# Nineteen slices for twenty in the last run of a pair of embedding fields

## The chip, the core and the metric

The kernel runs on one core of a Trainium2 chip. The metric is the device time of one execution in microseconds. The engines are named as in the profile: PE is TensorE (PEld its weight loads), DVE is VectorE, ACT is ScalarE, POOL is GpSimd and SP is SyncE, which here only issues DMAs.

## What is computed

A wide-and-deep recommender forward pass for 16384 rows. Cut to what matters:

```
tok = word_emb[token_idx].mean(axis=1)        # 32 rows of a 50000 x 300 table
e1, e2, e3 = emb_mhN[mhN_idx].mean(axis=1)    # 20 rows each of 1000, 5000, 10000 x 64 tables
o1, o2, o3, o4 = emb_ohN[ohN_idx]             # one row each of 100, 50, 20, 1000 x 64 tables
emb  = concatenate([tok, e1, e2, e3, o1, o2, o3, o4], axis=1)      # 748 columns
wide = sum of the looked-up wide_* weights of all seven small fields
h = relu(emb @ W1 + b1); h = relu(h @ W2 + b2); h = relu(h @ W3 + b3)   # 748-1024-512-256
return sigmoid(h @ Wd + bd + wide)
```

## The kernel before

**Tiles and steps.** The 16384 rows are 128 tiles of 128 rows. One Python loop over `step` (L710) writes the whole program out in order, under a manual schedule[...]. A tile has STEPS = 11 steps (`t, i = divmod(step, STEPS)`), and WAKE = 27 more steps follow the last tile, so there are 1435 steps.

**Four streams share the steps.**

- *Tokens* (`tokens`, L285). The 32 word rows of a tile's 128 samples are gathered by indirect DMAs that POOL issues (L300), two to a group of `tok_rows`, with six such buffers; three groups later DVE adds them up (`add_up`, L276, L278, L283). There are 4034 gathers: 32 to a tile, and in every second tile from the fifth on one fewer, because SP fetches that row set with plain DMAs (L335). Groups are paced (`tokens_by`, L670): two a step in the first 24 steps, then (2051 − 48) / (1435 − 24) = 1.42 a step.
- *Counts.* For the small fields DVE makes one-hot rows from the keys (`one_hots`, L394, two buffers of `hot`), ACT scales a part of them (L401), PE multiplies them into counts per table row, six pairs of samples a step (`counts`, L412; four in step 10), and ACT writes the counts to SBUF as `cnt` (L415).
- *Small sums* (`small_sums`, L427, matmul on L447) are the stream that the change touches. While step i of tile t makes the counts of t, PE multiplies the finished counts of tile t − 1 with the tables on the chip. The tables lie in n_h = 138 slices of 128 rows: e1 8, o4 8, e2 40, e3 79, o1, o2 and o3 one each. Fields go in pairs in the order of `SMALL`: (e1, o4) 16 slices, (e2, e3) 119, (o1, o2) 2, and (o3) 1. Each pair sums into one PSUM tile `pg` from a pool with a single buffer, `ps_g` (L124); after the pair's last slice the generator yields an `evict`, a DVE reduce from `pg` into the features `g` (L437). The next pair's first slice is the next call of the generator, and its matmul waits for that reduce, since it writes the same buffer.
- *Layers.* The MLP works on blocks of three tiles (two and one near the end: 32 blocks of three, 12 of two, 8 of one), matmul by matmul (L565), with its results drained by ACT (L576). `layers.to(target + ahead)` (L772) sets how many are emitted in a step; `ahead` is the number of slices that an even spread would have done by then less those done.

**The order within a step:** `one_hots` of the next step; `counts` of this one; the early run of slices (L739); transposes of features where due (L488); token groups (L763); layer matmuls (L772); the late run of slices (L778); then `flush(step)` (L779) emits the reduces that are due. A reduce from an early run is due in the same step, one from a late run a step later (the last argument of `run_sums`). In step 0, `wide_term` of the tile before (L455, L461) comes right after this flush.

**How many slices each step has** is the table that the change edits (L636 to L643). `large` is 119 / 6 rounded up, 20:

```
step         1    2 (late)   3    4    5    6    7    9   10 (late)
slices      16    20        20   20   20   20   20    2    1
```

These are 139 for 138 slices. Pair (e2, e3) has 119 and begins in step 2; it takes 20 there, 80 in steps 3 to 6 and 19 in step 7. The twentieth slice of step 7 is o1's. Step 9 then has o2 and o3, and step 10 finds nothing left.

Of the kernel before, what the change touches and what calls it, by code (L numbers as in the profile page):

```python
# [74 lines left out]
def kernel(  # L75
# [560 lines left out]
    n_of = {f: slices[f][1] - slices[f][0] for f in SMALL}  # L636
    sizes_of_pairs = [sum(n_of[f] for f in SMALL[i : i + 2]) for i in (0, 2, 4, 6)]
    large = -(-sizes_of_pairs[1] // 6)
    early_sums = {1: sizes_of_pairs[0], 9: sizes_of_pairs[2], **{i: large for i in range(3, 8)}}
    late_sums = {2: large, 10: sizes_of_pairs[3]}  # L640
    sums_done = [0]
    for i in range(STEPS):
# [67 lines left out]
    for step in range(n_steps):  # L710
        t, i = divmod(step, STEPS)
# [129 lines left out]
```

## Time and profile before

| what | value |
|---|---|
| three timed runs | 5158.36, 5164.18, 5163.98 us, median 5163.98 us |
| profiled execution, its own time | 5157.98 us |
| profiled execution, span from first to last instruction | 5156.2 us |
| mean granted TensorE clock | 0.989 |
| PE busy | 4809.1 us (93%), 36252 matmuls |
| PEld busy | 3716.6 us (72%) |
| DVE busy | 3754.0 us (73%) |
| ACT busy | 2757.7 us (53%) |
| POOL busy | 3819.6 us (74%), 4034 of its 4041 instructions gathers |
| DMA engines | 44% in most slices, mean 127 GB/s |

The profile is one execution, which was 6.0 us shorter than the median of the timed runs and as long as the shortest of them. "Busy" counts instructions only[...]. Ends of matmuls are modelled, so that neighbours overlap. In timeline rows the columns are start, duration, engine, line, operation, output and inputs, and in brackets the idle time ahead with what ended it; rows of one kind in a row are merged, with their number after x.

### The profile page before, as it was taken

Reading aid. Unit: us, or ns where it says so; the run is one execution under the profiler, and the core shown is the slowest. Engines: PE = TensorE matmul, PEld = TensorE weight load, DVE = VectorE, ACT = ScalarE, POOL = GpSimd, SP = SyncE. Lnnn points to the kernel's source line nnn. Section 1 sums busy time; section 2 is a strip of 40 time slices with the busy share of each in tenths; the row PEclk is TensorE's granted clock in tenths of the full one; section 3 lists DMA queues with packets and bytes.
Section 4 is the critical chain, followed back from the end, with each engine's and each line's share of the span. In section 5 each row is a group of like instructions: output and inputs, shape, how many; then the busy total and the mean of one; then the engine's idle time right before and its main releaser. Section 6 shows DMA issues by size and latency. Waiting matters only on the chain.

```text
span 5156.2 us, 119649 instructions
## 1 busy us (share of the span) xinstructions
PE 4809.1 (93%) x36252; PEld 3716.6 (72%) x36252; DVE 3754.0 (73%) x6664; ACT 2757.7 (53%) x3658; POOL 3819.6 (74%) x4041
## 2 busy tenths in 40 slices
PE   6799999999999999999999999999999999999999
PEld 4566676676676667666667766766767888888898
DVE  6777777777777777777777777777777777777774
ACT  6455555555555555555555555555555555555552
POOL 7777777777777777777777777777777777777775
PEclk8899999999999999999999999999999999999999
DMA  7444444444444444444444444444444444444443
GB/s 202 128 126 126 123 127 127 124 126 124 125 127 123 124 127 124 125 126 125 125 125 126 125 126 123 127 128 127 127 128 124 126 125 124 128 127 127 127 120 100
DMA packets 276178, 653.78 MB, mean 127 GB/s; under 512 B 136091, under 2 KB 144667, under 8 KB 275527
## 3 DMA queue, kind: packets, MB, share of 16 engines
q0 software_dynamic: 193632, 619.88, 44.4%
q1 hardware_dynamic: 81895, 26.25, 2.4%
q8 instruction: 283, 4.64, 0.4%
q14 instruction: 368, 3.01, 0.2%
HBM read 645.63 MB, written 0.07 MB: 125 GB/s over the span
## 4 chain that ended last, share of the span: by engine, by line
PE 83%; DVE 9%; DMA 3%; issue 2%; ACT 2%; POOL 1%; SPq 1%; DVEq 0%; POOLq 0%; ACTq 0%
PE ph L565 44%; PE pg L447 28%; PE pc L412 8%; DMA tok_rows<-in_word_emb_dram,it 3%; DVE g L437 2%; DVE hot L394 2%; DVE own L278 2%; DVE own L283 2%; PE pc L488 2%; POOL tok_rows L300 1%; PE po L597 1%; DVE x L492 1%; ACT cnt L415 1%; ACT hot L401 0%; SPq L335 0%
## 5 line engine op out<-in xcount | busy, mean ns | idle before, releaser
L300 POOL DMA_INDIRECT tok_rows<-in_word_emb_dram,it x4034 | 3818.7, 947 | 1309.7 <-issue 907.9
L447 PE MATMUL pg<-terms,cnt 128*128 128x195 bf16 x17664 | 1735.9, 248 | 206.1 <-DVE g L437 206.1
L401 ACT ACTIVATE hot<-hot 64x768 bf16<-64x768 bf16 (+1 forms) x1408 | 1155.4, 821 | 1443.4 <-DVE hot L394 1427.5
L394 DVE TENSOR_TENSOR hot<-own,sc 128x1656 bf16<-128x1656 bf16 (+1 forms) x1408 | 1393.5, 990 | 367.9 <-PE pc L412 306.3
L447 PEld LDWEIGHTS <-cnt 128*128 128x128 fp8e3 x17664 | 1520.7, 98 | 43.2 <-issue 26.7
L565 PE MATMUL ph<-x,w_sb 128*128 128x384 f32 (+5 forms) x4932 | 1489.6, 441 | 45.8 <-DVE x L492 44.9
L415 ACT ACTIVATE cnt<-pc 128x828 uint16<-128x828 f32 (+1 forms) x1408 | 1186.9, 843 | 642.2 <-PE pc L412 615.0
L565 PE MATMUL ph<-h,w_sb 128*128 128x384 f32 (+2 forms) x4160 | 1219.6, 433 | 0.0
L565 PEld LDWEIGHTS ph<-x,w_sb 128*128 128x128 f32 (+1 forms) x4932 | 839.7, 192 | 454.9 <-issue 102.7
L278 DVE TENSOR_TENSOR own<-own,tok_rows 128x300 f32<-128x300 f32 x1920 | 917.5, 478 | 82.9 <-DMA tok_rows<-in_word_emb_dram,it 18.6
L565 PEld LDWEIGHTS ph<-h,w_sb 128*128 128x128 f32 x4160 | 700.4, 190 | 351.5 <-issue 103.8
L412 PEld LDWEIGHTS <-hot 128*128 128x128 bf16 x8192 | 592.0, 98 | 466.4 <-issue 220.7
L283 DVE TENSOR_TENSOR own<-own,tok_rows 128x300 f32<-128x300 f32 x1792 | 856.6, 478 | 94.3 <-DMA tok_rows<-in_word_emb_dram,it 33.3
L412 PE MATMUL pc<-hot 128*128 128x138 bf16 x8192 | 727.9, 224 | 55.8 <-ACT hot L401 53.5
L437 DVE TENSOR_REDUCE g<-pg 128x130 f32<-128x390 f32 (+1 forms) x512 | 262.1, 512 | 523.6 <-PE pg L447 518.2
L576 ACT ACTIVATE h<-ph,b_sb 128x384 f32<-128x384 f32 (+2 forms) x723 | 378.8, 524 | 274.6 <-PE ph L565 263.9
L492 DVE TENSOR_TENSOR x<-pc,scale 128x768 f32<-128x768 f32 x127 | 120.8, 951 | 105.8 <-PE pc L488 105.4
L381 DVE COPY sc<-pc 128x512 bf16<-128x512 bf16 x64 | 44.2, 691 | 144.4 <-PE pc L377 139.0
L488 PE MATMUL pc<-ident,g 128*128 128x128 f32 x762 | 106.7, 277 | 9.9 <-ACT cnt L415 9.9
L488 PEld LDWEIGHTS pc<-ident,g 128*128 128x128 f32 x762 | 83.0, 142 | 21.1 <-ACT cnt L415 16.8
L597 PE MATMUL po<-h,wd_sb 128*1 128x384 f32 (+2 forms) x208 | 70.0, 426 | 4.0 <-ACT h L576 2.7
L276 DVE TENSOR_TENSOR own<-tok_rows 128x300 f32<-128x300 f32 x128 | 61.3, 479 | 7.6 <-DMA tok_rows<-in_word_emb_dram,it 3.7
(54 smaller groups left out, 397.0 us busy)
## 6 DMA issues: line engine op xcount, KB each, us to landing
fetched<-in_word_emb_dram SPq DMA_DIRECT2D x7936, 1.2 KB
tok_rows<-in_word_emb_dram,it POOLq DMA_INDIRECT x4034
ix<-in_idx_dram SPq DMA_DIRECT2D x128, 32.0 KB
w_sb<-in_W_dram SPq DMA_DIRECT2D x6, 512.0 KB
raw<-in_mh_dram SPq DMA_DIRECT2D x4, 682.5 KB
it<-in_idx_dram SPq DMA_DIRECT2D x64, 32.0 KB
w_sb<-in_W_dram SPq DMA_DIRECT2D x1, 2048.0 KB
column<-in_idx_dram SPq DMA_DIRECT2D x62, 0.5 KB
```

Source lines behind the costliest of these rows:

```text
L278: nc.vector.tensor_add(tok_sum, tok_sum, a)
L283: nc.vector.tensor_add(to, tok_sum, b)
L300: nc.gpsimd.indirect_dma_start(out=rows[-1], out_offset=None, in_=word, in_offset=bass.IndirectOffsetOnAxis(ap=it[:, j : j + 1], axis=0),)
L394: nc.vector.tensor_tensor(hot[:, 0 : 2 * rows, :].rearrange("p i (n d) -> p i n d", d=2), iota.rearrange("p (n d) -> p n d", d=2).unsqueez ...
L401: nc.scalar.activation(upper, upper, AF.Copy, scale=UPPER)
L412: nc.tensor.matmul(pc[:, k // n, at : at + n_h], hot[:, 2 * k, 0:P], hot[:, 2 * k + 1, :], start=True, stop=True)
L415: nc.scalar.activation(cnt[:, :, b : b + rows].rearrange("l h (g k) -> l h g k", g=2), pc[:, :, 0 : n * n_h].rearrange("l g (k h) -> l h g ...
L437: nc.vector.tensor_reduce(field_columns(features(t), pair), pg[:, 0:n, :].rearrange("p f (c d) -> p f d c", c=3), AX.X, ALU.add,)
L447: nc.tensor.matmul(pg[:, j, :], by_slice[:, h, :], terms[:, h, :], start=(h == h0), stop=(h == h1 - 1))
L488: nc.tensor.transpose(pt[:, j // n, j % n, :], g[:, c : c + P], ident)
L565: nc.tensor.matmul(to, weights[: src.shape[0], k, m * P : (m + 1) * P], src, start=(k == 0), stop=(k == len(srcs) - 1),)
L576: nc.scalar.activation(dst[:, m, 0:n], ph[:, 0:n], AF.Relu, bias=bias[:, m : m + 1])
```

## The change

One entry of the table becomes a remainder. Step 7 has 119 − 5·20 = 19 slices instead of 20; everything else in the source is as it was.

```diff
     large = -(-sizes_of_pairs[1] // 6)
-    early_sums = {1: sizes_of_pairs[0], 9: sizes_of_pairs[2], **{i: large for i in range(3, 8)}}
+    early_sums = {1: sizes_of_pairs[0], 9: sizes_of_pairs[2], **{i: large for i in range(3, 7)}}
+    early_sums[7] = sizes_of_pairs[1] - 5 * large
     late_sums = {2: large, 10: sizes_of_pairs[3]}
     sums_done = [0]
     for i in range(STEPS):
```

The numbers now add up to 138. Step 7 ends with e3's last slice, step 9 has o1 and o2, and the late run of step 10 has o3. The counts of `sums_done`, which set `ahead`, are 135 and 137 after steps 7 and 9 where they were 136 and 138; step 10 ends at 138 in both.

## The prediction

> **What bounds the kernel now.** I read the page first, section 1 and the groups of section 5.
>
> ```profile
> PE 4809.1 (93%) x36252; PEld 3716.6 (72%) x36252; DVE 3754.0 (73%) x6664; ACT 2757.7 (53%) x3658; POOL 3819.6 (74%) x4041
> ...
> L300 POOL DMA_INDIRECT tok_rows<-in_word_emb_dram,it x4034 | 3818.7, 947 | 1309.7 <-issue 907.9
> L447 PE MATMUL pg<-terms,cnt 128*128 128x195 bf16 x17664 | 1735.9, 248 | 206.1 <-DVE g L437 206.1
> ```
>
> PE looks like the bound at 93%. Its largest idle time by far, 206.1 us, stands ahead of slice matmuls and ends with the pair reduce. The total of waits says how often:
>
> ```profile
> PE pg L447 <- DVE g L437: 206.1, 259, 6.2
> ```
>
> 259 times is twice per tile (128 tiles) and three more. The timeline of one tile shows both places, step 9 of one tile and step 7 of the next:
>
> ```profile
> 2503.62 0.24 PE L447 MATMUL pg<-terms,cnt 128*128 128x195 bf16 x1
> 2503.91 0.57 DVE L437 TENSOR_REDUCE g<-pg 128x130 f32<-128x390 f32 x1 [0.21 <-PE pg L447]
> 2504.53 0.24 PE L447 MATMUL pg<-terms,cnt 128*128 128x195 bf16 x1 [0.66 <-DVE g L437]
> ...
> 2535.60 1.80 PE L447 MATMUL pg<-terms,cnt 128*128 128x195 bf16 x19
> 2537.43 0.56 DVE L437 TENSOR_REDUCE g<-pg 128x130 f32<-128x390 f32 x1 [0.90 <-PE pg L447]
> 2538.05 0.24 PE L447 MATMUL pg<-terms,cnt 128*128 128x195 bf16 x1 [0.65 <-DVE g L437]
> ```
>
> In step 7, 19 slices run, PE stands while DVE empties `pg`, then o1's slice runs alone. In step 9, o2 runs, PE stands again, and o3 follows. All layer matmuls of the step queue behind.
>
> POOL at 74% looks idle, but its timeline is a fixed beat. The first and last gathers of the run, and one from the middle with its neighbour:
>
> ```profile
> 3.00 1.10 POOL L300 DMA_INDIRECT tok_rows<-in_word_emb_dram,it  x1 [1.52 <-DMA it<-in_idx_dram]
> ...
> 2499.11 0.94 POOL L300 DMA_INDIRECT tok_rows<-in_word_emb_dram,it  x1 [0.30 <-issue]
> 2500.36 0.95 POOL L300 DMA_INDIRECT tok_rows<-in_word_emb_dram,it  x1 [0.30 <-issue]
> ...
> 5128.90 0.95 POOL L300 DMA_INDIRECT tok_rows<-in_word_emb_dram,it  x1 [0.30 <-issue]
> ```
>
> A gather is 0.95 us and 0.30 us always stand ahead of it, whatever is named as releaser: 1.25 us. The windows of 250 us, which hold 200 beats, tell how full POOL is:
>
> ```profile
> core 0: us, POOL busy (x), PEclk, DMA share, GB/s
> 1000.00:1250.00 250.00, 185.18 (x196) 0.99 0.47 125
> 3500.00:3750.00 250.00, 189.29 (x200) 1.00 0.48 127
> ```
>
> From 3500 to 3750 not one beat is missed; elsewhere 2 to 5 of 200 are. From 5080.11 to 5128.90, 39 beats take 48.79 us, 1.251 each. So 4033 beats need 5041 to 5045 us, and took 5128.90 − 3.00 = 5125.90: **POOL has only 81 to 85 us of slack in the whole run.** Two engines are nearly full, and the change relieves one.
>
> [...] `pg` has one buffer, and the 0.66 us are what it costs here. [...]20 in a row take 1.89 us, (1.89 − 0.25) / 19 = 0.086 each.
>
> **The change part by part.**
>
> *Removed: two stands per tile.* In step 7 the twentieth slice would follow at 2535.60 + 19 · 0.086 = 2537.24 and starts at 2538.05: 0.81 us. In step 9 o3 would follow o2 at 2503.71 and starts at 2504.53: 0.82. Per tile 1.63, times 128 = 209 us of PE time. The longer waits of the first 250 us (25.5 us over 8 in that window's waits) add perhaps 20, which I leave out: they belong to the conversion of the tables. After the change both places hold other work: step 7 goes from e3 into the layers, step 9 from o2 into the layers.
>
> *Moved: o1 by two steps, o3 by most of one.* No instruction is added or dropped. In the built instruction order POOL's gathers and SP's DMAs stand as before, so no queue of theirs is passed. On PE o1's matmul passes the counts of steps 8 and 9, o3's those of step 10 and that step's layers. `ahead` rises by one unit in steps 7 to 9; a layer matmul of a block of three counts as 7.5, so one matmul moves by a step now and then: nothing.
>
> *Two waits in place of two.* o3's matmul now waits for the (o1, o2) reduce. That ends at about 2504.5, and o3 comes at the end of step 10, about 2510.5 in this tile: 6 us of cover (the layers of step 9, the counts and layers of step 10). Cost nothing; bound above by the 0.82 of now, if the cover is gone. Next, (e1, o4)'s first slice waits for o3's reduce, which has moved on DVE from step 9 to the end of step 0, behind the adds, directly ahead of L455:
>
> ```profile
> 2510.95 0.48 DVE L283 TENSOR_TENSOR own<-own,tok_rows 128x300 f32<-128x300 f32 x1
> ...
> 2511.33 0.15 DVE L455 TENSOR_REDUCE wide<-g 128x1 f32<-128x6 f32 x1
> ...
> 2514.73 1.54 PE L447 MATMUL pg<-terms,cnt 128*128 128x195 bf16 x16
> ```
>
> The reduce (0.36 us) would end near 2511.8 and the slices start at 2514.73: 2.9 us of cover, the layers of step 0. Where a block ends there are none in steps 0 and 1, and PE comes at once; then the wait is at most: one-hot rows done, four adds of 0.51 and the reduce, 2.40, less ACT's 0.84 and six count matmuls' 0.3 on PE's side, 1.3 us. I take 0.36 us for each of the 52 blocks, 19 us of PE time: DVE has that much more ahead of the next one-hot rows. Behind the waiting slices on PE are the layers and counts of step 1; ACT waits for those. Below nothing neither wait can go.
>
> *The sum.* PE alone: 5156.2 − 209 + 19 = 4966 us. POOL alone: the span less 81 to 85, about 5073 us; its start (3.0) and the tail after the last gather (26.4: landing, adds, the last block) stay. **The larger ends last: 5073.** To it I add what POOL would still miss. Where it is the bound already (3500 to 3750) it misses none; at the end, where single-tile blocks make PE's tiles long (16-slice runs at 5013.37 and 5053.68, 40.3 us, against POOL's 11 steps · 1.42 groups · 2 − 0.5 = 30.7 gathers · 1.25 = 38.4), PE without the stands still needs 38.7 plus 0.4, about 0.7 a tile over 8 tiles, 5 us, partly taken up by six buffers of rows. With 5 us the span is 5078, the execution's own time (span + 1.8) 5080. That execution was 6.0 us under the median of the runs and equal to their shortest; runs differ by 6 for no reason shown, so I add 4: **5084 us**.
>
> Where do the other 120 us of PE time go? Into new waits: once PE is ahead of the tokens, DVE [...] waits for gathered rows with the one-hot rows behind it, and PE waits for these.
>
> **The rivals.**
>
> - *A, the forecast*: POOL's beat takes over, 5084.
> - *B, half of it*: PE still falls behind in stretches (ends of blocks, the first 500 us) by more than six buffers can bridge, so that half of POOL's 83 us stay: 5164 − 42 = 5122. For it: POOL's misses now come in lumps of up to 3.0 us. Against: the 0.7 us per tile by which PE was late (83 / 128) are less than half of the 1.63 won.
> - *C, the beat is no bound*: the 0.30 us shrink under pressure and PE's 209 us come through whole: 5164 − 209 = 4955. Against: 1.25 holds even in the first 40 us, when nothing else is waited for.
> - *D, the waits are only handed on* (o3 and then (e1, o4) meet unfinished reduces, 0.8 each): 5164. Against: 6 and 2.9 us of cover.
> - *E, slower*: the reduce of o3, at its new place behind four adds in step 0, holds PE ahead of the 16 slices in every tile for 1.3 us, and o3 itself still waits 0.82 in step 10. 2.12 against 1.63 is 0.5 more on each of 128 tiles, 63 us: 5227. It decides from 1.63 us per tile on. It needs PE without layers in steps 10 to 1 of every tile, where the trace has them in all but the last tile of a block.
>
> **How the numbers follow.** A 0.70, B 0.17, C 0.04, D 0.05, E 0.04. The range holds A with its unknowns (POOL missing nothing, on the level of the shortest run: 5074; a miss of 20 us and the level of the longest: 5100) and is carried on through B's middle to 5130, C and the rest left out: 5072 to 5130. Faster by over 0.2% (10 us, about what a measurement of this kernel can tell from no change): A, B and C, 0.91; within 0.2%: D, 0.05; slower: E, 0.04.
>
> **What would show it.** Right: POOL at 199 or 200 gathers in nearly all windows of 250 us; no lone slice after a run of 19; waits of PE for L437 well below 206 us; in their place PE waiting for L401's one-hot rows and DVE for gathered rows; PE's share of busy time a little up, its idle time still over 200 us. Wrong: POOL still missing 3 beats in 200 (B or D), gathers closer than 1.25 us (C), or 16-slice runs with a wait of over a microsecond for L437 in most tiles (E).

## The result, and the profile after

The changed kernel takes **5080.89 us** (median of five runs, 5080.07 to 5081.92). The kernel before took 5161.22 us in five runs (5158.36 to 5164.18). The ratio is 0.9845, with a 95% interval from 0.9832 to 0.9859: 80 us less. The forecast was 5084 us.

The profiled execution took 5081.92 us, with a span of 5080.2 us. The same lines of the page as were shown of before (`...` stands for lines left out, here and below):

```profile
PE 4817.1 (95%) x36252; PEld 3732.6 (73%) x36252; DVE 3728.4 (73%) x6664; ACT 2739.9 (54%) x3658; POOL 3817.9 (75%) x4041
...
L300 POOL DMA_INDIRECT tok_rows<-in_word_emb_dram,it x4034 | 3817.0, 946 | 1230.5 <-issue 779.0
...
L447 PE MATMUL pg<-terms,cnt 128*128 128x195 bf16 x17664 | 1723.8, 249 | 36.8 <-DVE g L437 36.4
```

The idle time ahead of the slices fell from 206.1 to 36.8 us. Yet PE's idle time in all, the span less its busy time, fell only from 347 to 263 us. The total of waits says what stands there now (waiting engine and line, what ended the wait, us in total, times, longest):

```profile
DVE own L283 <- DMA tok_rows<-in_word_emb_dram,it: 380.4, 581, 2.8
...
DVE g L437 <- PE pg L447: 208.8, 163, 4.1
...
DVE own L278 <- DMA tok_rows<-in_word_emb_dram,it: 201.3, 284, 4.0
...
DVE hot L394 <- PE pc L412: 113.8, 119, 4.8
...
PE pc L412 <- ACT hot L401: 79.5, 67, 4.6
...
PE pg L447 <- DVE g L437: 36.4, 29, 2.6
```

DVE's waits for gathered rows on L283 and L278 were 33.3 and 18.6 us in the kernel before; they are 380.4 and 201.3 now. Its waits for PE (518.2 and 306.3 before) are 208.8 and 113.8. So PE was late for DVE before, and the gathers are late for DVE now. The wait that costs PE the most in all has become that for one-hot rows, 79.5 us for 53.5.

The page also follows the chain of work that ended last back from the last instruction and gives each engine its share of the span. Before, and then after:

```profile
PE 83%; DVE 9%; DMA 3%; issue 2%; ACT 2%; POOL 1%; SPq 1%; DVEq 0%; POOLq 0%; ACTq 0%
```

```profile
PE 50%; DMA 18%; DVE 12%; issue 9%; POOL 6%; SPq 2%; ACT 2%; DVEq 0%; POOLq 0%; ACTq 0%
```

The 3% and the 18% of DMA are gathered rows. Half of the chain still runs through PE, but of the 33 points that left PE, 20 went to these rows and to POOL, which issues the gathers.

The windows of 250 us show POOL (busy time, gathers touched, granted clock, DMA share, GB/s):

```profile
core 0: us, POOL busy (x), PEclk, DMA share, GB/s
1000.00:1250.00 250.00, 189.04 (x200) 0.99 0.48 128
```

Between 1000 and 1250 there were 196 gathers, now there are 200, as many as fit; from 3500 to 3750 it was full already. First and last gather of the run:

```profile
2.92 1.10 POOL L300 DMA_INDIRECT tok_rows<-in_word_emb_dram,it  x1 [1.44 <-DMA it<-in_idx_dram]
...
5048.04 0.95 POOL L300 DMA_INDIRECT tok_rows<-in_word_emb_dram,it  x1 [0.30 <-issue]
```

That is 5045.12 us for 4033 beats, 1.2510 each, where before it was 5125.90 us. The gathers took 80.8 us less. The spans of the two profiled executions differ by 76.0, so this is the whole gain and a little more; what was lost again at the end is looked at below.

The two places that the change edits, in the tile that corresponds to the one shown of before:

```profile
2492.75 0.33 PE L447 MATMUL pg<-terms,cnt 128*128 128x195 bf16 x2
...
2492.91 2.77 PE L565 MATMUL ph<-h,w_sb 128*128 128x384 f32 x8
...
2499.32 0.26 PE L447 MATMUL pg<-terms,cnt 128*128 128x195 bf16 x1
...
2500.15 1.54 PE L447 MATMUL pg<-terms,cnt 128*128 128x195 bf16 x16
...
2527.66 1.80 PE L447 MATMUL pg<-terms,cnt 128*128 128x195 bf16 x19
...
2529.29 1.48 PE L565 MATMUL ph<-x,w_sb 128*128 128x384 f32 x4
```

Step 9 has o1 and o2 and goes straight on into eight layer matmuls; step 7 goes from its nineteenth slice into four. o3, alone at 2499.32, and the 16 slices of the next pair 0.83 us later start with no bracket, that is without a wait, although this tile ends a block and there are only counts in between.

### The profile page after: what moved, and what is told of

The parts are those of the page before. It is cut to its first block, busy times and chain, and to the rows that moved or that the text cites. A ratio compares the mean times of both kernels' runs of the same rounds, so it can differ in the third digit from the quotient of the medians.

```text
span 5080.2 us, 119649 instructions
## 1 busy us (share of the span) xinstructions
PE 4817.1 (95%) x36252; PEld 3732.6 (73%) x36252; DVE 3728.4 (73%) x6664; ACT 2739.9 (54%) x3658; POOL 3817.9 (75%) x4041
## 4 chain that ended last, share of the span: by engine, by line
PE 50%; DMA 18%; DVE 12%; issue 9%; POOL 6%; SPq 2%; ACT 2%; DVEq 0%; POOLq 0%; ACTq 0%
PE ph L565 26%; DMA tok_rows<-in_word_emb_dram,it 18%; PE pg L447 18%; POOL tok_rows L300 6%; PE pc L412 5%; DVE hot L394 4%; DVE own L283 3%; DVE own L278 2%; SPq L335 1%; PE pc L488 1%; ACT hot L401 1%; DVE x L492 1%; DVE g L437 1%; ACT cnt L415 1%; SPq L326 0%
## 5 line engine op out<-in xcount | busy, mean ns | idle before, releaser
L447 PE MATMUL pg<-terms,cnt 128*128 128x195 bf16 x17664 | 1723.8, 249 | 36.8 <-DVE g L437 36.4
L394 DVE TENSOR_TENSOR hot<-own,sc 128x1656 bf16<-128x1656 bf16 (+1 forms) x1408 | 1394.4, 990 | 196.3 <-PE pc L412 113.8
L415 ACT ACTIVATE cnt<-pc 128x828 uint16<-128x828 f32 (+1 forms) x1408 | 1187.7, 844 | 343.1 <-PE pc L412 324.1
L283 DVE TENSOR_TENSOR own<-own,tok_rows 128x300 f32<-128x300 f32 x1792 | 857.4, 478 | 427.9 <-DMA tok_rows<-in_word_emb_dram,it 380.4
L278 DVE TENSOR_TENSOR own<-own,tok_rows 128x300 f32<-128x300 f32 x1920 | 918.1, 478 | 258.3 <-DMA tok_rows<-in_word_emb_dram,it 201.3
L412 PE MATMUL pc<-hot 128*128 128x138 bf16 x8192 | 732.0, 225 | 88.2 <-ACT hot L401 79.5
L576 ACT ACTIVATE h<-ph,b_sb 128x384 f32<-128x384 f32 (+2 forms) x723 | 379.5, 525 | 139.4 <-PE ph L565 124.2
L437 DVE TENSOR_REDUCE g<-pg 128x130 f32<-128x390 f32 (+1 forms) x512 | 259.8, 507 | 210.3 <-PE pg L447 208.8
L492 DVE TENSOR_TENSOR x<-pc,scale 128x768 f32<-128x768 f32 x127 | 120.9, 952 | 54.9 <-PE pc L488 52.6
L276 DVE TENSOR_TENSOR own<-tok_rows 128x300 f32<-128x300 f32 x128 | 61.5, 480 | 53.7 <-DMA tok_rows<-in_word_emb_dram,it 50.7
L488 PEld LDWEIGHTS pc<-ident,g 128*128 128x128 f32 x762 | 85.3, 145 | 15.9 <-ACT cnt L415 14.2
```

The lines of the kernel that those rows point to most:

```text
L278: nc.vector.tensor_add(tok_sum, tok_sum, a)
L283: nc.vector.tensor_add(to, tok_sum, b)
L394: nc.vector.tensor_tensor(hot[:, 0 : 2 * rows, :].rearrange("p i (n d) -> p i n d", d=2), iota.rearrange("p (n d) -> p n d", d=2).unsqueez ...
L412: nc.tensor.matmul(pc[:, k // n, at : at + n_h], hot[:, 2 * k, 0:P], hot[:, 2 * k + 1, :], start=True, stop=True)
L415: nc.scalar.activation(cnt[:, :, b : b + rows].rearrange("l h (g k) -> l h g k", g=2), pc[:, :, 0 : n * n_h].rearrange("l g (k h) -> l h g ...
L437: nc.vector.tensor_reduce(field_columns(features(t), pair), pg[:, 0:n, :].rearrange("p f (c d) -> p f d c", c=3), AX.X, ALU.add,)
```

## The experiments

My theory: the change takes about 200 us of stands (waits of PE between two instructions) off PE, and the time falls only until POOL's beat of gathers is the bound. Its rival: the time follows PE's stands one for one, and the stands were worth 80 us. Two further questions came from the profile after: why the tail after the last gather grew, and whether the beat is now all that holds the kernel.

Four kernels ran twice. Their first runs fell on a chip on which the kernel before took 7374 us, so the answers come from the second runs. On the chips of e5 to e12 the kernel before ran again and agrees with its first time within 2 us; the changed kernel did not, so comparisons with its 5080.89 us go from chip to chip.

| run | what it is | kernel before on that chip | this | ratio and interval |
|---|---|---|---|---|
| e1_stand7 | stand of step 7 kept | 7373.99 | 7336.74 | 0.9938, 0.9915 to 0.9962 |
| e2_stand9 | stand of step 9 kept | 7373.99 | 7327.12 | 0.9931, 0.9910 to 0.9952 |
| e3_before_fewer | before, 128 gathers fewer | 7373.99 | 7234.20 | 0.9804, 0.9782 to 0.9825 |
| e4_after_fewer | changed, 128 gathers fewer | 7373.99 | 7147.05 | 0.9706, 0.9679 to 0.9734 |
| e5_warm_tail | changed, 56 matmuls in the tail | 5162.09 | 5092.23 | 0.9866, 0.9851 to 0.9881 |
| e6_more_fetched | changed, 11 gathers to SP | 5162.09 | 5081.49 | 0.9844, 0.9831 to 0.9857 |
| e7_both | both | 5162.09 | 5080.87 | 0.9843, 0.9829 to 0.9856 |
| e8_before_fewer | as e3 | 5162.97 | 5156.97 | 0.9987, 0.9980 to 0.9994 |
| e9_after_fewer | as e4 | 5162.97 | 4960.60 | 0.9604, 0.9588 to 0.9620 |
| e10_stand7 | as e1 | 5162.38 | 5089.36 | 0.9856, 0.9841 to 0.9871 |
| e11_stand9 | as e2 | 5162.38 | 5113.58 | 0.9907, 0.9892 to 0.9922 |
| e12_better | changed, 28 matmuls and 11 gathers to SP | 5162.38 | 5064.30 | 0.9810, 0.9797 to 0.9823 |

### Two stands, and a chip that was no use for them

The first four kernels, against the kernel before (e1) or the changed one (e2):

```diff
e1, e10, on the kernel before:
-    early_sums = {1: sizes_of_pairs[0], 9: sizes_of_pairs[2], **{i: large for i in range(3, 8)}}
+    early_sums = {1: sizes_of_pairs[0], 9: sizes_of_pairs[2] - 1, **{i: large for i in range(3, 8)}}
e2, e11, on the changed kernel:
-    early_sums = {1: sizes_of_pairs[0], 9: sizes_of_pairs[2], **{i: large for i in range(3, 7)}}
+    early_sums = {1: sizes_of_pairs[0], 9: sizes_of_pairs[2] + sizes_of_pairs[3], **{i: large for i in range(3, 7)}}
...
-    late_sums = {2: large, 10: sizes_of_pairs[3]}
+    late_sums = {2: large}
e3, e8 on the kernel before; e4, e9 on the changed kernel:
                     j = q * TOK_GROUP + r
+                    if j == 0:
+                        continue
...
-                under_way.append((t, q, rows))
+                under_way.append((t, q, rows if len(rows) == TOK_GROUP else rows * TOK_GROUP))
```

> One half of the change undone: step 7 keeps its twentieth slice (o1, which meets the reduce of e2 and e3), step 9 has o2 alone, step 10 has o3. One stand per tile is left. My theory (the gather beat of 1.25 us is the bound, and before the change PE was late by only 83 us / 128 = 0.65 us per tile): the 0.82 us won in step 9 cover nearly all of it, so 5085 to 5100 us, with POOL missing under 1 beat in 200. Rival (the time follows PE's stands one for one): half of the gain, 5121 us.

> The other half undone: step 7 has 19 slices, step 9 has o1, o2 and o3, so that o3 meets the reduce of o1 and o2 there, and step 10 has none. One stand per tile is left, at another place. My theory: as with the other half, 5085 to 5100 us, the place doesn't matter. Rival (one for one): 5121 us. A second rival, that the new place of o3 at the end of step 10 costs something: then this kernel is no slower than the changed one, 5081 us or less.

> The kernel before with one gather fewer in every tile (3906 for 4034): the row of token 0 is left out, and that of token 1 is added in its place, so that VectorE's adds stay. GpSimd's beat needs 128 x 1.25 = 160 us less. My theory (with the stands PE is nearly full, so fewer gathers buy little): 5120 to 5160 us. Rival (the gathers alone are the bound): 5161 - 160 = 5001 us.

> The changed kernel with the same gather left out of every tile (token 0's row replaced by token 1's). GpSimd alone would need 3906 x 1.251 + 34 = 4920 us, PE alone about 4966 us by the sum of the prediction. My theory: PE becomes the bound, 4960 to 4990 us, and the difference to the kernel before with fewer gathers is the whole price of the stands, 150 to 200 us, about double the 80 us of the change itself. Rival (PE was never more than 80 us from its own floor, the gathers don't limit): 5070 to 5081 us, the same difference as with all gathers.

Measured: 7337, 7327, 7234 and 7147 us, with 7374 for the kernel before. The profile of e1_stand7 shows waits that the profile of the kernel before, from another chip, doesn't have. The total of waits has PE stand 533.3 us ahead of the slices for nothing that the profile shows, ACT ahead of L415 1254.5 us and DVE ahead of L394 968.4 us for what it only calls remote, and in the window POOL is far from its beat:

```profile
PE pg L447 <- issue: 533.3, 676, 5.0
```

```profile
1000.00:1250.00 250.00, 133.69 (x141) 0.88 0.34 91
```

With 141 gathers in 250 us instead of 200, nothing can be read here of a bound by gathers. (Leaving out 128 gathers won 140 us from the kernel before on this chip; on another, below, it won 6.) None of the four expectations is tested by these runs. What ended those waits the profile doesn't say.

### With fewer gathers: the whole price of the stands

> The kernel before with one gather fewer in every tile, as e3_before_fewer, which ran on a chip where the kernel before took 7374 us[...], so that it told nothing of the balance between PE and GpSimd. Token 0's row is left out, and token 1's is added in its place. My theory (with the stands PE is nearly full): 5120 to 5160 us, where GpSimd alone would be done by about 5001 us. Rival (the gathers alone are the bound): 5001 us.

> The changed kernel with the same gather left out of every tile, as e4_after_fewer, on another chip. My theory: PE becomes the bound, 4960 to 4990 us, and the difference to the kernel before with fewer gathers is the whole price of the stands, 150 to 200 us, about double the 80 us of the change itself. Rival (the gathers don't limit the changed kernel): 5070 to 5081 us, and the same difference as with all gathers.

Measured: **5156.97 and 4960.60 us.** Taking 160 us of gathers from the kernel before won 6 us (ratio 0.9987); e9 is 120 us below the changed kernel. Both theories' numbers were far apart, and mine hold: 5120 to 5160, and 4960 to 4990. The difference of the two, 196 us, is what the stands cost where gathers don't limit, 196 / 256 = 0.77 us for each of two per tile. The waits of e8_before_fewer (its line numbers are two higher) and then of e9_after_fewer:

```profile
PE pg L449 <- DVE g L439: 203.5, 259, 5.8
```

```profile
PE pg L449 <- DVE g L439: 12.2, 11, 2.7
```

PE's stands are the same 259 as in the kernel before, though POOL has 128 gathers less to do. POOL has much room in the first and a little in the second: its 3905 beats would take 4897 us at 1.254 us, the beat of both executions (more of it below), and took 5122 in e8 and 4930 in e9. That PE is the bound of e9 is also what its chain says, with PE 83% and DMA 3% as in the kernel before. But DVE still waits 121 us for gathered rows in e9 (L276, L278 and L283), so PE's own floor may lie a little under 4961, and the price of the stands a little over 196.

So two limits lie close together: PE with its stands at 5157 us, the gathers at 5081, PE without stands at about 4961. The change moved the kernel from the first to the second and left 120 us of the 196 unused. That is shown for whole kernels; that the unused part turned into waits for gathered rows is read from the waits and the chain of the profile after.

### One stand at a time

> The stand in step 7 kept, that in step 9 gone, as e1_stand7, on another chip. With fewer gathers the two stands of all tiles cost 5157 - 4961 = 196 us, and PE's own floor with both is about 5157 us. With one of them it is 5157 - 98 = 5059 us, below the 5080 us of the gather beat. My theory: 5080 to 5092 us, as fast as the changed kernel or nearly, since the beat takes over. Rival (the time follows PE's stands one for one): half of the gain, 5121 us.

> The stand in step 9 kept, that in step 7 gone, as e2_stand9, on another chip. My theory: 5080 to 5092 us, as with the other half. Rival (one for one): 5121 us. If the new place of o3 at the end of step 10 cost something, this kernel would be faster than the changed one.

Measured: **5089.36 us** (5086.17 to 5095.29) and **5113.58 us** (5110.69 to 5116.95). With the stand of step 7 kept, 73 of the 80 us are won, as my theory has it; one for one would have been half. Its profiled execution, 5095.29 us, had its first gather at 3.00 and its last at 5062.47, 1.2545 for each of 4033 beats, so nearly all that it lost against the changed kernel's it lost by a slower beat, of which more below. With the stand of step 9 kept, only 49 are won. My range ended at 5092, the rival's number was 5121: here my expectation failed. Part of this is the beat too. The gathers of e11's profiled execution (5111.68 us) run from 3.00 to 5079.19, and each takes 0.949 us on average, as in e10, for 0.946 in the changed kernel: some 12 us of the 30 that it is slower than the changed kernel's. The other 18 or so are missed beats. Against e10's, with the same beat, it is 16.4 us slower. The waits of e10_stand7 and then of e11_stand9:

```profile
PE pg L447 <- DVE g L437: 118.1, 139, 4.6
```

```profile
PE pg L447 <- DVE g L437: 156.5, 131, 6.3
```

About as many stands in both, but 0.85 us each on average with step 7's and 1.19 us with step 9's. The timeline shows two of them, first a stand of step 9 in e11_stand9, then one of step 7 in e10_stand7:

```profile
2633.75 0.33 PE L447 MATMUL pg<-terms,cnt 128*128 128x195 bf16 x2
2633.84 0.73 DVE L394 TENSOR_TENSOR hot<-own,sc 128x1104 bf16<-128x1104 bf16 x1
...
2635.12 0.47 DVE L283 TENSOR_TENSOR g<-own,tok_rows 128x300 f32<-128x300 f32 x1
...
2635.51 0.55 DVE L437 TENSOR_REDUCE g<-pg 128x130 f32<-128x390 f32 x1
...
2636.11 0.24 PE L447 MATMUL pg<-terms,cnt 128*128 128x195 bf16 x1 [2.04 <-DVE g L437]
```

```profile
2537.47 1.80 PE L447 MATMUL pg<-terms,cnt 128*128 128x195 bf16 x19
...
2539.31 0.56 DVE L437 TENSOR_REDUCE g<-pg 128x130 f32<-128x390 f32 x1 [2.94 <-PE pg L447]
...
2539.93 0.25 PE L447 MATMUL pg<-terms,cnt 128*128 128x195 bf16 x1 [0.66 <-DVE g L437]
```

In step 7 the run of 19 slices takes 1.8 us, DVE gets through its queue meanwhile and stands ready ahead of the reduce (its bracket names PE), so that PE waits 0.66 us. In step 9 there are only two slices. DVE still has the one-hot rows of step 10 and the two adds of a group to do, the second of them shown, the reduce queues behind them, and PE waits 2.04 us. That long it isn't always: 44 of the 127 stands of step 9 in e11 are under 0.7 us, and 49 are over 1.2. In the kernel before, 96 of 128 were under 0.7. That they were short because PE had stood in step 7 and DVE had caught up by then is my reading; no run tests it alone. The end of o3 in step 10 costs little: in the changed kernel 21 waits with 24.5 us in all stand ahead of the 16 slices that follow it, and e11_stand9, which avoids them, is still the slower one.

### The tail, and rows fetched by SyncE

In the changed kernel the stretch after the last gather takes longer, 5080.2 − 5049.0 = 31.2 us, where it was 5156.2 − 5129.85 = 26.4. In the profile before, and then after, the last block's first layer:

```profile
5133.29 0.55 PE L488 MATMUL pt<-ident,g 128*128 128x128 f32 x3 [1.82 <-DVE g L283]
...
5139.45 4.18 PE L565 MATMUL ph<-x,w_sb 128*128 128x128 f32 x36
```

```profile
5051.49 0.90 PE L488 MATMUL pt<-ident,g 128*128 128x128 f32 x3 [7.52 <-DVE g L283]
...
5061.32 6.24 PE L565 MATMUL ph<-x,w_sb 128*128 128x128 f32 x36
```

PE, no longer behind, stands 7.52 us for the last row, and then the same 36 matmuls take 6.24 us for 4.18. From these transposes to the first matmul of the second layer it is 10.2 us before and 15.9 after, 5.7 more; they come 0.9 us sooner after the last gather; together that is the 4.8 us of the tail. The windows show the clock that PE was granted meanwhile:

```profile
core 0: us, PE busy (x), PEclk, DMA share, GB/s
5051.00:5056.00 5.00, 3.41 (x13) 0.50 0.00 0
5056.00:5061.00 5.00, 4.47 (x19) 0.50 0.00 0
```

In the kernel before it was 1.00 in the same layer (5133 to 5139). There PE had stood 1.82 us, here 7.52, and the clock fell within that stand: 1.00 from 5044 to 5048, 0.59 from 5048 to 5051, 0.50 from 5051 to 5064. Which length of stand is needed these lines don't show.

```diff
e5 and e7 (56) and e12 (28), ahead of the last transposes:
+    warm = ps_h.tile([P, N], F32, name="warm", tag="ph")
+    for _ in range(56):
+        nc.tensor.matmul(warm[:, 0:P], w1_sb[:, 0, 0:P], ident, start=True, stop=True)
     for _, k, ks in waiting:
         block = block_for(k)
e6, e7, e12:
-FETCH_STEPS = 20
+FETCH_STEPS = 19
...
-    fetches = [(int(summed_at(t)) - FETCH_AHEAD, t) for t in range(FETCH_FROM, tiles, 2)]
+    fetches, at = [], int(summed_at(FETCH_FROM)) - FETCH_AHEAD
+    for t in range(FETCH_FROM, tiles):
+        if int(summed_at(t)) - FETCH_AHEAD >= int(at):
+            fetches.append((int(at), t))
+            at += 19.25
```

> The changed kernel with 56 needless matmuls (128 x 128, float32, into a PSUM buffer that nobody reads) put on PE ahead of the last three transposes, where PE stands 7.5 us for the last token row and then runs slowly: 36 layer matmuls took 6.24 us there, 4.18 us in the kernel before, which stood only 1.8 us. Theory (the tail after the last gather is 31.2 us for 26.4 because PE's clock falls while it stands): 36 matmuls take 4.2 us again and the time falls by 3 to 5 us, to about 5077 us. Rival (the tail is longer for another reason, such as DMA landing or the order of the layers): 5081 us or more.

> The changed kernel with SyncE fetching a row set every 19.25 steps instead of every 22 (73 tiles for 62), so that GpSimd issues 4023 gathers instead of 4034. Theory (the gather beat is the bound, nothing else): 11 x 1.25 = 14 us less, 5067 us. Rival (SyncE, with 62 us of issues in each 67 us, comes late and VectorE waits for fetched rows): 5081 us or more. The same output is computed.

> Both of these edits on the changed kernel: more rows fetched by SyncE, and the needless matmuls ahead of the last transposes. Theory: the two add up, since one shortens the beat's part and the other the tail: 5063 us. Rival: either of them fails as its own rival says.

Measured: medians of 5092.23, 5081.49 and 5080.87 us, none below the changed kernel by more than 0.02. But the single runs lie in two heaps: e6 ran once in 5071.03 us and four times in 5080.18 to 5081.99, e5 once in 5081.49 and three times in 5091.07 to 5093.45. The last gathers of the profiled executions, of e6 (5071.03 us) and then of e7 (5081.57 us), say where that comes from; the first ones start at 2.90 and 2.92:

```profile
5036.01 0.95 POOL L300 DMA_INDIRECT tok_rows<-in_word_emb_dram,it  x1 [0.30 <-issue]
```

```profile
5046.56 0.94 POOL L300 DMA_INDIRECT tok_rows<-in_word_emb_dram,it  x1 [0.30 <-DVE own L283]
```

The same 4022 beats take 5033.11 us in the one, 1.2514 each, and 5043.64 us in the other, 1.2540. In these executions **the beat itself has two values**, 0.2% apart; it isn't that more beats are missed, for starts over 1.3 us apart are 23 in e6 and 20 in e7. On the pages a gather takes 947 ns on average in e6 and 949 in e7, which is nearly all of the difference. Only profiled executions show their beat. At the beat of 1.251, e6 is 11 us faster than the changed kernel's profiled execution (5081.92 us at 1.2510): the 14 expected, less 3. The expectation of e6 is nearly met there, and its rival, SyncE coming late, is not seen: DVE waits for fetched rows once, for 0.3 us. That the four slower runs had the slower beat fits in size (4022 · 0.0026 = 10.5 us) but isn't shown.

e5 had the right cause and the wrong size. Its 36 matmuls took 4.18 us again, but the 56 needless ones took 12.67 us (the profile shows each of them as two, x112), and the transposes after them began 5.3 us later than in the changed kernel, counted from the start; the profiled execution took 5081.49 us, no gain. e7 has the same 56 and the slower beat, so it says nothing of whether the two edits add up. With half as many:

> The changed kernel with 11 more row sets fetched by SyncE (73 tiles for 62) and with 28 needless matmuls instead of 56 ahead of the last three transposes: the profile counts a float32 matmul of 128 x 128 twice, so that 56 took 12.7 us and were 5.3 us too long. Theory: 28 take 6.3 us of the 7.5 us of standing, PE then runs 36 matmuls in 4.2 us for 6.2 us, and the time is 5081 - 14 - 5 = 5062 us at a gather beat of 1.251 us; at the beat of 1.254 us that other executions had, 12 us more, 5074 us. Rival: the end isn't set by PE's clock, 5067 and 5079 us.

Measured: **5064.30 us** (5064.01 to 5066.88), ratio 0.9810, where the changed kernel has 0.9845. The profiled execution took 5066.88 us. Its end:

```profile
5034.87 6.42 PE L803 MATMUL warm<-ident,w_sb 128*128 128x128 f32 x56
...
5047.56 4.18 PE L565 MATMUL ph<-x,w_sb 128*128 128x128 f32 x36
```

The transposes follow at 5041.44 with no wait, the granted clock is 1.00 from 5041 to 5047, and from the last gather's end at 5038.3 to the end of the span (5065.1) it is 26.8 us, 4.4 less than in the changed kernel. The beat was 1.2517 here. Expected were 5062 us, by the rival (the end isn't set by PE's clock) 5067: the median lies between them and the profiled execution at the rival's, so the time alone doesn't decide. The traces do: the gathers take 10.8 us less than in the changed kernel and the tail 4.4. The profiled execution of e6, which lacks only the needless matmuls and had nearly the same beat, is 4.2 us slower, and its tail has 32.3 us. This is the version to keep.

## Why the prediction was right, step by step

*The two stands per tile cost 0.81 us each, 209 in all.* Right in size: 196 us between e8_before_fewer and e9_after_fewer, against the 190 left after the 19 for ends of blocks. Wrong as a rule that both cost alike: kept alone, the stand of step 9 costs more than that of step 7 (waits of 1.19 us on average for 0.85), since its reduce then often queues behind DVE's work (in the tile shown PE waits 2.04 us).

*PE alone would need 4966 us.* The nearest measurement is e9_after_fewer, with 4960.6, where POOL is not quite out of the way.

*POOL's beat leaves 81 to 85 us.* Right: the gathers took 80.8 us less, and the beat was 1.2510, as in the kernel before.

*POOL would still miss about 5 us, mostly at the end.* Too much. 5045.12 us for 4033 beats of 1.250 to 1.251 leaves 0 to 4 us; the starts over 1.3 us apart add up to 2.8. At the end PE wasn't late, as the step had it, but 7.5 us early.

*The tail of 26.4 us stays.* This step was wrong: it grew to 31.2, since PE waits there (7.52 us) and its granted clock then is 0.50. The two errors have opposite signs, and the span came out at 5080.2 for 5078. That the forecast is only 3 us off is in part luck: the bound alone gave a span of 5073, and the terms of 4 to 5 us added to it partly made up for the tail.

*The level: 4 us added for runs above the profiled one.* Not needed. The runs after lie within 2 us, and the profiled one is their longest. Without it the forecast would have been 5080.

*Moved waits cost nothing, or 0.36 us at ends of blocks.* Right in the sum. The waits for the reduce are 36.4 us over 29 times in the whole run; the 21 ahead of the 16 slices are 24.5 us, where the sum had 19 us for 52. The bound of 1.3 us for one of them was too low: the longest is 2.49. The tile shown, which ends a block, has none.

*Where the rest of PE's time goes.* Right for DVE and in size: DVE waits 582 us for gathered rows on L278 and L283 where it waited 52, and PE's idle time is 263 us, "still over 200". Only in part right in the place: of some 85 us of new waits of PE, 26 are for one-hot rows, and most of the rest are at the layers, for ACT (L576) and DVE (L492). The clock took a part that the prediction doesn't have: the mean granted clock fell from 0.989 to 0.981, and PE's busy time rose by 8 us for the same matmuls.

The rivals: half of the gain (5122) and the handed-on waits (5164) are excluded by the result, the shrinking beat (4955) by the beat of 1.2510, and the slower case (5227) by the result and by o3 and the next pair starting without a wait.

## What to carry to other kernels

An engine at 74% can be a full one, as POOL was with 0.95 us of every 1.25 busy: look at the starts of its instructions, and if they come on a fixed beat, count the beats that are missed, for these are all that a change elsewhere can win as long as the beat stays. Where two engines are nearly full, price the stand on the one, then find the floor of the other; the gain is at most the smaller of the two, and taking load off the second engine in both kernels shows the rest. With one accumulation buffer, let a group end where other work follows on the same engine, and expect a stand there to cost what is queued ahead of the drain, not only the drain (2.04 us for 0.66 in the two shown).

## What was not expected of the hardware

- The beat of gathers on GpSimd is constant to 0.1% over the changed kernel's run (1.2505 to 1.2515 us in stretches of 500 us), but differed between executions on one chip: 1.2514 and 1.2540 us for the same 4022 beats. On 5070 us this is 10.5 us, as much as the edits of e6 bring. Of the ten traces with the kernel before at about 5162 us, five show a mean gather of 946 or 947 ns and five one of 949 or 950, with both kinds on each of two chips. What sets it is open. Medians of a kernel that is bound by it can hide such an edit.
- A stand of 7.5 us on PE made what followed slow: the granted clock was 0.50, 36 matmuls took 6.24 us for 4.18, and with 28 needless float32 matmuls in its place they took 4.18 again and the tail is 4.4 us shorter. Shorter stands came ahead of a low clock in one tile and not in another: in two tiles of the kernel before, PE waited 0.71, about 0.36 and 1.45 us in quick order, and the 8 layer matmuls after that took 2.85 us at a granted clock of 1.00 in the one and 4.54 us at 0.62 in the other. In the clock records of the kernel before and of the changed one every stretch at half clock, but for the one at the end of the run, lasts 3.41 us or a whole multiple of it (18 stretches before, 29 after): 110 us in all before, 191 after, with the one at the end.
- One chip ran the kernel before in 7374 us, and the four kernels traced there have long waits that the profile gives to no instruction of the kernel: 525 to 622 us on PE ahead of the slices, 1192 to 1483 us on ACT ahead of the line that writes `cnt`, 942 to 1244 us on DVE ahead of the one-hot rows. What stood behind that is open.
